# The last group of an MLP pipeline: layer 1 first, three second-layer tiles held back, and a shorter last norm

## The chip, the core and the metric

The kernel runs on one core of a Trainium2 chip. Its time is the time on the device in microseconds (us), a median of several runs. One further execution is recorded by the hardware profiler; the profile and the trace below are of that execution. Engines are named as the profile names them: PE is TensorE (PEld its weight loads), DVE is VectorE, ACT is ScalarE, POOL is GpSimd and SP is SyncE, which only issues transfers here.

## The reference, cut to what matters

The input x has 16 x 512 rows of 512 numbers, 8192 rows in all. Each row is normalized in several ways, the results are put side by side, and a two-layer network with a final norm is added back to x:

```python
h = _ln(x, pw_g[pathway_ids], pw_b[pathway_ids])
h = _ln(h, cp_g[compartment_ids], cp_b[compartment_ids])
t = _ln(x, tm_g[time_steps], tm_b[time_steps])
m, n, r = (x + _mlp_ln(state, ...)[:, None, :] for state in (memory, noise, resource))
s = _ln(x, ms_g[scale_type], ms_b[scale_type])
cat = jnp.concatenate([w[0] * h, w[1] * t, w[2] * m, w[3] * n, w[4] * r, w[5] * s], axis=-1)
# _mlp_ln(cat, ...): silu(cat @ int_W1 + b1) @ int_W2 + b2, then _ln with int_g, int_be
return x + _mlp_ln(cat, int_W1, int_b1, int_W2, int_b2, int_g, int_be)
```

All of it is in float32.

## The kernel before, in words

**Tiling.** The 8192 rows are first ordered by their pair of compartment and scale type, and then go through in 16 groups ("windows") of 512 rows. A group has four tiles of 128 rows. The first layer is folded into three products for each tile, all into one PSUM tile: block X (x itself, with the matrix `wx_` for the three broadcast states), block V (the normalized x, with a matrix for the tile's pair, for t and s together) and block H (the twice normalized h, with `wh_`). So a group is 12 first-layer tile products and 4 second-layer ones. Each is four chunks of the 512-long sum, and each chunk is two PE instructions of 128x512.

**What a group needs.** The V matrix of a tile is made in two steps. `s_part` (line 190) writes four scaled chunks on ACT, and `build` (line 196) adds a scaled second matrix to each chunk on DVE. There are two buffers for these matrices, `vs[0]` and `vs[1]`, used in turn, so the third and fourth tile of a group take the buffers of the first and second once PE has read them, chunk by chunk. Each PE product waits for its chunk alone. The H block comes from the "front": `front_a` (normalized x on ACT, line 237; then DVE lines 260 to 265 and a power on POOL, line 269), `front_b1` (line 147 on DVE, line 276 on ACT) and `front_b2` (line 289 and a blockwise transpose, line 156, on DVE). `spread` then has SP issue 16 transfers (line 164) that lay the transposed blocks out as PE needs them. The hidden values go the same way: `hidden` (add on DVE, line 309; silu on ACT, line 312), `turn_z` (transpose on DVE), `spread`.

**The end of a group.** `layer2` (line 324) is the second product. `last_a` adds the bias on DVE (line 327) and sums the squares on ACT (line 332). `last_std` takes the variance on DVE (line 340) and the power -1/2 on POOL (line 345). `last_b` scales by it and by the gain (line 353), then adds the row (line 354), both on DVE. `put_out` is an indirect transfer issued by POOL (line 358); each one waits until the one before it has landed. The mean needs no work here, because the means of the second matrix's rows were taken out beforehand. `shift_x` (line 294, POOL) adds the norm's offset to the stored x. `gather_add` (line 130, POOL) fetches the first layer's row offsets.

**The order.** It is written out by hand; each engine runs its instructions in the order in which the code gives them. `step(s, older, prev, st, nx, nn)` is one of 16 steps of a group: `st` is the group in its first layer, `prev` the one before it, which is in its second layer, `older` the one before that, whose outputs are being stored. Steps 0 to 3 are the four X tiles, steps 4 to 11 alternate a V tile of `st` with a second-layer tile of `prev`, steps 12 to 15 are the H tiles. The norm of `prev` is finished for all four tiles at once (one power of 128x4) while the H tiles run. After group 15, its own second layer stands alone: `end_hidden` (last hidden tile, transposes, 16 transfers), and then four times `layer2`, `last_a`, `last_std`, `last_b`, `put_out` (lines 990 to 999). There are three buffers for x (`xbs`), used by the groups in turn; PSUM has four tiles for the first layer and four for the second.

Of the kernel before, what the change touches and what calls it, by code (L numbers as in the profile page):

```python
# [8 lines left out]
F32 = mybir.dt.float32  # L9
I32 = mybir.dt.int32  # L10
AF = mybir.ActivationFunctionType
ALU = mybir.AluOpType
AX = mybir.AxisListType

P = 128
# [37 lines left out]
def kernel(ctx: ExitStack, tc: tile.TileContext, a: dict, out: bass.AP):  # L53
# [23 lines left out]
    nc = tc.nc  # L77
    B, S, D = a["x"].shape
    NT = B * S
    NJ = S // P  # L80
    NC = D // P
    NW = NT // S
    Q = 4
# [11 lines left out]
    gp = ctx.enter_context(tc.tile_pool(name="gp", bufs=3))  # L95
# [16 lines left out]
    vs = [const.tile([P, NC, D], F32, name=f"vs{k}") for k in range(2)]  # L112
# [3 lines left out]
    yb = const.tile([P, NJ, D], F32, name="yb")  # L116
    rows = const.tile([P, 3, D], F32, name="rows")
# [11 lines left out]
    def gather(dst, table, idx, **kw):  # L129
        nc.gpsimd.indirect_dma_start(dst, None, table, bass.IndirectOffsetOnAxis(ap=idx, axis=0), **kw)  # L130
# [20 lines left out]
    def rot_tile(blk, name):  # L151
        return catp.tile([P, Q, NC, NJ, L], F32, tag=f"rot{blk}", name=name)

    def turn(rot, j, src):

        nc.vector.transpose(rot[:, :, :, j, :].rearrange("p q c t -> p c q t"),  # L156
                            src.rearrange("p (c q t) -> p c q t", c=NC, q=Q))

    def spread_row(st, rot, cat, blk, g):

        if cat not in st:
            st[cat] = catp.tile([P, Q, NC, P], F32, tag=f"cat{blk}", name=f"{cat}{st['w']}")
        for q in range(Q):
            nc.sync.dma_start(st[cat][q * L : (q + 1) * L, g].rearrange("p c t -> p (c t)"),  # L164
                              st[rot][g * L : (g + 1) * L, q].rearrange("p c j t -> p (c j t)"))

    def spread(st, blk):
        for g in range(Q):
            spread_row(st, "r" + blk, "c" + blk, blk, g)
# [12 lines left out]
        gather(cp, cp_rows[:, :], i_cp[:, j, w : w + 1])  # L182
        st["g", j] = pw, cp

    def s_part(st, g):

        w = st["w"]
        st["v", g] = v = vs[(Q * w + g) % 2]
        for c in range(NC):
            nc.scalar.activation(v[:, c], ws[:, c], AF.Identity, scale=scs[:, c, g, w : w + 1])  # L190

    def build(st, g):
        w = st["w"]
        v = st["v", g]
        for c in range(NC):
            nc.vector.scalar_tensor_tensor(v[:, c], wt[:, c], sct[:, c, g, w : w + 1], v[:, c], ALU.mult, ALU.add)  # L196

    def gather_add(st, g):
        w = st["w"]
        st["add", g] = t = gp.tile([P, D], F32, tag="add", name=f"add{w}_{g}", bufs=4)  # L200
        gather(t, rows_2[:, :], i_add[:, g, w : w + 1])
# [39 lines left out]
    def turn_to(st, rot, blk, j, src):  # L241
        if rot not in st:
            st[rot] = rot_tile(blk, f"{rot}{st['w']}")
        turn(st[rot], j, src)
# [10 lines left out]
    def norm_n(st, j):  # L255
        st["xn", j] = norm(st, j, "rs", "nm", "xn")

    def front_1(st, j):
        pw, _ = st["g", j]
        nc.vector.tensor_mul(pw[:, :D], st.pop(("xn", j)), pw[:, :D])  # L260
        nc.vector.tensor_add(pw[:, :D], pw[:, :D], pw[:, D:])
        st["mv", j] = mv = small.tile([P, 1, 2], F32, tag="mvh", name="mvh")
        stats(mv, 0, pw[:, :D], P, "h")
        st["ve", j] = ve = small.tile([P, 1], F32, tag="veh", name="veh")
        nc.vector.tensor_scalar_add(ve, mv[:, :, 1], EPS)  # L265

    def front_pow(st, j):
        st["rs", j] = rs = small.tile([P, 1], F32, tag="rsh", name="rsh")
        nc.gpsimd.tensor_tensor(rs, st.pop(("ve", j)), mhalf[:, :1], ALU.pow)  # L269

    def front_mean(st, j):
        st["nm", j] = neg_mean(st.pop(("mv", j)), st["rs", j], 1, "h")

    def front_norm(st, j):
        pw, _ = st["g", j]
        nc.scalar.activation(pw[:, :D], pw[:, :D], AF.Identity, bias=st.pop(("nm", j)), scale=st.pop(("rs", j)))  # L276

    def front_a(st, j):
        norm_n(st, j)
        front_1(st, j)  # L280
        front_pow(st, j)

    def front_b1(st, j):
        front_mean(st, j)
        front_norm(st, j)

    def front_b2(st, j):
        pw, cp = st.pop(("g", j))
        nc.vector.tensor_mul(pw[:, :D], pw[:, :D], cp)  # L289
        turn_to(st, "rH", "H", j, pw[:, :D])  # L290

    def shift_x(st, j):

        nc.gpsimd.tensor_add(st["xb"][:, j, :], st["xb"][:, j, :], rows[:, 2, :])  # L294


    def psum(k, name):
        return (ps_1, ps_2)[k].tile([P, D], F32, tag=("p1", "p2")[k], name=name)

    def layer1(st, blk, g):  # L300
        if blk == "X":
            st["p1", g] = psum(0 if st["w"] == 0 else 1, f"p1_{st['w']}_{g}")
        m = {"X": wx_, "V": st.get(("v", g)), "H": wh_}[blk]
        for c in range(NC):
            nc.tensor.matmul(st["p1", g], st["c" + blk][:, g, c, :], m[:, c, :],  # L305
                             start=(blk == "X" and c == 0), stop=(blk == "H" and c == NC - 1))

    def hidden_add(st, g):
        nc.vector.tensor_add(st["add", g], st["p1", g], st["add", g])  # L309

    def hidden_silu(st, g):
        nc.scalar.activation(st["add", g], st["add", g], AF.Silu)  # L312

    def hidden(st, g):
        hidden_add(st, g)
        hidden_silu(st, g)

    def turn_z(st, g):
        turn_to(st, "rZ", "Z", g, st["add", g])

    def layer2(st, j):
        st["p2", j] = p2 = psum(0, f"p2_{st['w']}_{j}")
        for c in range(NC):
            nc.tensor.matmul(p2, st["cZ"][:, j, c, :], w2[:, c, :], start=(c == 0), stop=(c == NC - 1))  # L324

    def last_add(st, j):
        nc.vector.tensor_add(yb[:, j, :], st["p2", j], rows[:, 0, :])  # L327

    def last_sum(st, j):
        if "ssy" not in st:  # L330
            st["ssy"] = small.tile([P, NJ], F32, tag="ssy", name="ssy", bufs=2)
        nc.scalar.activation(junk, yb[:, j, :], AF.Square, accum_out=st["ssy"][:, j : j + 1])  # L332

    def last_a(st, j):
        last_add(st, j)
        last_sum(st, j)

    def last_var(st, lo=0, hi=NJ):
        st["vey"] = ve = small.tile([P, NJ], F32, tag="vey", name="vey")[:, lo:hi]
        nc.vector.tensor_scalar(ve, st["ssy"][:, lo:hi], 1.0 / D, EPS, ALU.mult, ALU.add)  # L340

    def last_pow(st, lo=0, hi=NJ):
        if lo == 0:
            st["rsy"] = small.tile([P, NJ], F32, tag="rsy", name="rsy")
        nc.gpsimd.tensor_tensor(st["rsy"][:, lo:hi], st["vey"], mhalf[:, lo:hi], ALU.pow)

    def last_std(st, lo=0, hi=NJ):
        last_var(st, lo, hi)
        last_pow(st, lo, hi)

    def last_b(st, j):
        y = yb[:, j, :]
        nc.vector.scalar_tensor_tensor(y, y, st["rsy"][:, j : j + 1], rows[:, 1, :], ALU.mult, ALU.mult)  # L353
        nc.vector.tensor_add(y, y, st["xb"][:, j, :])

    def put_out(st, j):
        w = st["w"]
        nc.gpsimd.indirect_dma_start(out_rows, bass.IndirectOffsetOnAxis(ap=tok[:, j, w : w + 1], axis=0),  # L358
                                     yb[:, j, :], None)
# [51 lines left out]
    at = 0  # L411
# [197 lines left out]
    sts = [{"w": w, "xb": xbs[(w + 2) % 3], "tok": (tok, w)} for w in range(NW)] + 2 * [None]  # L609
# [37 lines left out]
    _, bcol = row_col(bpos, NG, "b")  # L647
# [207 lines left out]
    def home(w, blk):  # L855
# [8 lines left out]
    }  # L864
    for_tile = {
        "gx": lambda st, j: gather_x(st, (j,)), "gh": gather_h, "xs": x_sums, "sp": s_part, "bd": build, "nv": norm_v, "tx": turn_x, "xn": norm_n,
        "f1": front_1, "fp": front_pow, "fm": front_mean, "fn": front_norm, "f2": front_b2, "ga": gather_add,
        "ha": hidden_add, "hs": hidden_silu, "tz": turn_z, "l2": layer2, "la": last_add, "lq": last_sum,
        "lb": last_b, "po": put_out, "sh": shift_x,
    }  # L870
# [22 lines left out]
    def end_hidden(st, older):  # L893

        last_b(older, 3)
        hidden(st, 3)
        turn_z(st, 2)
        turn_z(st, 3)
        spread(st, "Z")
# [83 lines left out]
        if s in (5, 6, 7, 8):  # L983
            shift_x(st, s - 5)

    for w in range(2, NW):
        for s in range(16):
            step(s, *sts[w - 2 : w + 3])

    older, prev = sts[NW - 2 : NW]  # L990
    put_out(older, 2)
    end_hidden(prev, older)
    put_out(older, 3)
    for j in range(NJ):
        layer2(prev, j)
        last_a(prev, j)
        last_std(prev, j, j + 1)
        last_b(prev, j)
        put_out(prev, j)


# [51 lines left out]
```

## Time and profile before

The median is 1050.83 us over 3 runs (1048.07 to 1051.16).

| profiled execution of the kernel before | us |
|---|---|
| its own device time | 1051.53 |
| span from its first to its last instruction | 1049.4 |
| PE busy | 998.2 |
| DVE busy | 873.8 |
| ACT busy | 572.8 |
| POOL busy | 568.5 |

The page of a profile gives the busy time of each engine, the span in 40 slices, the groups of instructions with the mean duration of one, and the idle time before them with the instruction that ended it ("<-DMA cZ<-rZ": a transfer from rZ to cZ ended it). Further views of the trace list instructions in order of time ("start, duration, engine, line, operation, output<-input, count [idle before <-releaser]"; "SPq" is a transfer that SP issues), or tell for chosen stretches how busy each engine was, and which TensorE clock was granted as a share of full speed.

### The profile page before, as it was taken

What the parts mean: (1) busy time and instruction counts of PE and PEld (TensorE: products, weight loads), DVE (VectorE), ACT (ScalarE), POOL (GpSimd) and SP (SyncE); (2) the same over time, 40 slices, a digit from 0 to 9 for tenths busy, and PEclk for the clock granted to TensorE, in tenths of its full rate; (3) what the DMA queues carried; (4) which work ended last, traced back from release to release, by engine and by line L of the source; (5) the groups of instructions that cost most, each with busy time, mean ns of one, the idle gap of its engine ahead of it and who ended that gap; (6) DMA issues with size and microseconds to landing.
All of it is one profiled execution on the core that took longest, in us unless ns stands there. A gap on an engine that the chain in (4) does not pass through costs nothing.

```text
span 1049.4 us, 11007 instructions
## 1 busy us (share of the span) xinstructions
PE 998.2 (95%) x2523; PEld 452.1 (43%) x2523; DVE 873.8 (83%) x1574; ACT 572.8 (55%) x1153; POOL 568.5 (54%) x570
## 2 busy tenths in 40 slices
PE   6989699899999999999999999999999999999976
PEld 5634244343344444444444444444444444444432
DVE  8878789888889898888888888888888888898643
ACT  3689774473746474637464646555464737463311
POOL 4764651645656564737464646465655556563412
PEclk9979899899999999999999999999999999999998
DMA  9685887666767585857676666767666767675412
GB/s 282 205 261 161 230 246 223 164 182 184 199 184 211 165 224 153 234 154 221 173 208 173 196 180 202 191 184 191 196 186 195 194 195 196 185 209 145 131 53 67
DMA packets 95655, 197.66 MB, mean 188 GB/s; under 512 B 26290, under 2 KB 26290, under 8 KB 95592
## 3 DMA queue, kind: packets, MB, share of 16 engines
q0 software_dynamic: 32096, 108.55, 35.8%
q1 hardware_dynamic: 62230, 87.44, 29.9%
q10 hardware_dynamic: 1266, 0.99, 0.3%
q8 instruction: 21, 0.34, 0.1%
q14 instruction: 42, 0.34, 0.1%
HBM read 104.14 MB, written 21.44 MB: 120 GB/s over the span
## 4 chain that ended last, share of the span: by engine, by line
PE 78%; DVE 8%; DMA 4%; ACT 4%; issue 3%; SPq 1%; POOL 1%; POOLq 0%; DVEq 0%; ACTq 0%
PE p L305 55%; PE p L324 17%; PE pe L811 3%; PE pn L574 2%; SPq L164 1%; DVE vs L196 1%; ACT vs L190 1%; DMA add<-rows,i_add 1%; DMA xbs<-in_mem_W 1%; PE ph L549 1%; DVE yb L353 1%; ACT pw L276 1%; DMA out<-yb,tok 1%; POOL xbs L130 1%; DVE pw L289 1%
## 5 line engine op out<-in xcount | busy, mean ns | idle before, releaser
L305 PE MATMUL p<-vs,cV 128*128 128x512 f32 x512 | 233.1, 599 | 5.8 <-DVE vs L196 5.8
L324 PE MATMUL p<-w,cZ 128*128 128x512 f32 x512 | 231.5, 597 | 7.1 <-DMA cZ<-rZ 7.1
L305 PE MATMUL p<-wx__82,cX 128*128 128x512 f32 x512 | 227.2, 602 | 2.0 <-DVE add L309 2.0
L305 PE MATMUL p<-wh__83,cH 128*128 128x512 f32 x512 | 222.8, 592 | 0.0
L196 DVE SCALAR_TENSOR_TENSOR vs<-wt,sct,vs 128x512 f32<-128x512 f32 x256 | 209.3, 876 | 0.0
L190 ACT ACTIVATE vs<-ws,scs 128x512 f32<-128x512 f32 x256 | 163.4, 707 | 2.7 <-PE pe L811 2.1
L269 POOL TENSOR_TENSOR rsh<-veh,mhalf 128x1 f32<-128x1 f32 x64 | 45.9, 718 | 203.2 <-DVE veh L265 195.3
L305 PEld LDWEIGHTS p<-vs,cV 128*128 128x128 f32 x512 | 97.7, 192 | 131.9 <-issue 96.8
L324 PEld LDWEIGHTS p<-w,cZ 128*128 128x128 f32 x512 | 98.0, 192 | 131.2 <-issue 130.5
L305 PEld LDWEIGHTS p<-wx__82,cX 128*128 128x128 f32 x512 | 98.7, 193 | 126.7 <-issue 119.5
L305 PEld LDWEIGHTS p<-wh__83,cH 128*128 128x128 f32 x512 | 97.3, 190 | 122.5 <-issue 122.0
L276 ACT ACTIVATE pw<-pw,nmh,rsh 128x512 f32<-128x512 f32 x64 | 51.8, 810 | 130.5 <-DVE nmh L147 130.5
L312 ACT ACTIVATE add<-add 128x512 f32<-128x512 f32 x64 | 40.3, 630 | 145.9 <-DVE add L309 145.9
L358 POOL DMA_INDIRECT out<-yb,tok x64 | 67.8, 1059 | 65.5 <-DVE yb L353 24.3
L332 ACT ACTIVATE junk<-yb 128x512 f32<-128x512 f32 x64 | 40.1, 627 | 98.0 <-DVE yb L327 98.0
L130 POOL DMA_INDIRECT add<-rows,i_add x64 | 75.9, 1186 | 24.2 <-issue 9.2
L260 DVE TENSOR_TENSOR pw<-xn,pw 128x512 f32<-128x512 f32 x64 | 44.0, 688 | 48.5 <-ACT xn L237 48.5
L294 POOL TENSOR_TENSOR xbs<-xbs,rows 128x512 f32<-128x512 f32 x64 | 81.4, 1274 | 0.9
L130 POOL DMA_INDIRECT cp<-cp_rows,i_cp x64 | 67.9, 1061 | 19.5 <-issue 19.2
L130 POOL DMA_INDIRECT xbs<-in_x,tok x64 | 64.9, 1015 | 24.2 <-issue 18.0
L130 POOL DMA_INDIRECT pw<-in_pw,i_pw x64 | 63.9, 999 | 22.4 <-issue 12.7
L237 ACT ACTIVATE xm<-xbs,mnm,mrs 128x512 f32<-128x512 f32 x64 | 48.7, 804 | 40.5 <-DVE rV L156 40.5
(228 smaller groups left out, 1220.5 us busy)
## 6 DMA issues: line engine op xcount, KB each, us to landing
cX<-rX SPq DMA_DIRECT2D x256, 64.0 KB
cV<-rV SPq DMA_DIRECT2D x256, 64.0 KB
cH<-rH SPq DMA_DIRECT2D x256, 64.0 KB
cZ<-rZ SPq DMA_DIRECT2D x256, 64.0 KB
cVe<-rVe SPq DMA_DIRECT2D x64, 64.0 KB
rows<-adde SPq DMA_DIRECT2D x14, 256.0 KB
w1x<-in_int_W SPq DMA_DIRECT2D x2, 1024.0 KB
ws<-in_int_W SPq DMA_DIRECT2D x1, 1024.0 KB
```

The lines of the kernel that those rows point to most:

```text
L130: nc.gpsimd.indirect_dma_start(dst, None, table, bass.IndirectOffsetOnAxis(ap=idx, axis=0), **kw)
L190: nc.scalar.activation(v[:, c], ws[:, c], AF.Identity, scale=scs[:, c, g, w : w + 1])
L196: nc.vector.scalar_tensor_tensor(v[:, c], wt[:, c], sct[:, c, g, w : w + 1], v[:, c], ALU.mult, ALU.add)
L237: nc.scalar.activation(t, st["xb"][:, j, :], AF.Identity, bias=st[nm][:, j : j + 1], scale=st[rs][:, j : j + 1])
L260: nc.vector.tensor_mul(pw[:, :D], st.pop(("xn", j)), pw[:, :D])
L269: nc.gpsimd.tensor_tensor(rs, st.pop(("ve", j)), mhalf[:, :1], ALU.pow)
L276: nc.scalar.activation(pw[:, :D], pw[:, :D], AF.Identity, bias=st.pop(("nm", j)), scale=st.pop(("rs", j)))
L294: nc.gpsimd.tensor_add(st["xb"][:, j, :], st["xb"][:, j, :], rows[:, 2, :])
L305: nc.tensor.matmul(st["p1", g], st["c" + blk][:, g, c, :], m[:, c, :], start=(blk == "X" and c == 0), stop=(blk == "H" and c == NC - 1))
L312: nc.scalar.activation(st["add", g], st["add", g], AF.Silu)
L324: nc.tensor.matmul(p2, st["cZ"][:, j, c, :], w2[:, c, :], start=(c == 0), stop=(c == NC - 1))
L358: nc.gpsimd.indirect_dma_start(out_rows, bass.IndirectOffsetOnAxis(ap=tok[:, j, w : w + 1], axis=0), yb[:, j, :], None)
```

## The change

The steps of the last group (`st` = group 15) are written out in a function of their own, `last_window`. The loop over `step` ends one group earlier.

- The order of PE's tiles in the last group was X X X X, V P V P V P V P, H H H H, then Z Z Z Z (P is a second-layer tile of group 14, Z one of group 15). It becomes X X X X, V V V V, P, H H H H, P P P, Z Z Z Z.
- The V matrix of the third tile is written into the x buffer of group 13, which is no longer needed. That of the fourth goes into the first tile's buffer. On DVE, the builds of the third and fourth matrix follow the front of tile 3 directly; the first of them is issued after the SP transfers for H.
- The last two stores of group 13 stay in steps 1 and 2, but are issued at the head of the step, ahead of the power on POOL instead of behind it. The gathers of the row offsets come in steps 3 to 6 instead of 3, 4, 7, 8, and the four `shift_x` in steps 4 to 7 instead of 5 to 8.
- The transposed hidden values of group 15 use the buffers of block V, since those of block Z still hold group 14's.
- The norm of both last groups is finished tile by tile, by `finish`. A multiplication by the gain (line 994) is placed behind the bias add; a single instruction (line 996) then scales by the power and adds the row. The two instructions of `last_b` depended on the power both.

```diff
-    def s_part(st, g):
+    def s_part(st, g, at=None):
-        st["v", g] = v = vs[(Q * w + g) % 2]
+        st["v", g] = v = vs[(Q * w + g) % 2] if at is None else at
...
-    def turn_z(st, g):
-        turn_to(st, "rZ", "Z", g, st["add", g])
+    def turn_z(st, g, blk="Z"):
+        turn_to(st, "rZ", blk, g, st["add", g])
...
-    for w in range(2, NW):
+    def last_window(older, prev, st):
+
+        def finish(done, j):
+
+            y = yb[:, j, :]
+            layer2(done, j)
+            last_a(done, j)
+            yg = gp.tile([P, D], F32, tag="cp", name=f"yg{done['w']}_{j}")
+            nc.vector.tensor_mul(yg, y, rows[:, 1, :])
+            last_std(done, j, j + 1)
+            nc.vector.scalar_tensor_tensor(y, yg, done["rsy"][:, j : j + 1], done["xb"][:, j, :], ALU.mult, ALU.add)
+            put_out(done, j)
+
+        for s in range(13):
+            if s == 8:
+                finish(prev, 0)
+            if s < 12:
+                layer1(st, "XVH"[s // 4], s % 4)
+            if s == 0:
+                end_hidden(prev, older)
+            elif s == 1:
+                put_out(older, 2)
+                front_a(st, 2)
+                s_part(st, 2, older["xb"])
+            elif s == 2:
+                put_out(older, 3)
+                front_b1(st, 2)
+                front_a(st, 3)
+                front_b2(st, 2)
+            elif s == 3:
+                front_b1(st, 3)
+                build(st, 1)
+                front_b2(st, 3)
+                spread(st, "H")
+                build(st, 2)
+            elif s == 5:
+                s_part(st, 3, vs[Q * st["w"] % 2])
+            elif s == 6:
+                build(st, 3)
+            elif s >= 9:
+                hidden(st, s - 9)
+                if s >= 10:
+                    turn_z(st, s - 10, "V")
+            if 3 <= s < 7:
+                gather_add(st, s - 3)
+            if 4 <= s < 8:
+                shift_x(st, s - 4)
+        turn_z(st, 3, "V")
+        for g in range(Q):
+            spread_row(st, "rZ", "cZ", "V", g)
+        for j in range(1, NJ):
+            finish(prev, j)
+        for j in range(NJ):
+            finish(st, j)
+
+    for w in range(2, NW - 1):
         for s in range(16):
             step(s, *sts[w - 2 : w + 3])
-
-    older, prev = sts[NW - 2 : NW]
-    put_out(older, 2)
-    end_hidden(prev, older)
-    put_out(older, 3)
-    for j in range(NJ):
-        layer2(prev, j)
-        last_a(prev, j)
-        last_std(prev, j, j + 1)
-        last_b(prev, j)
-        put_out(prev, j)
+    last_window(*sts[NW - 3 : NW])
```

## The prediction

> **What bounds the kernel now.** I read the page first, then the last 90 us in order of time, engine by engine.
>
> ```profile
> span 1049.4 us, 11007 instructions
> PE 998.2 (95%) x2523; PEld 452.1 (43%) x2523; DVE 873.8 (83%) x1574; ACT 572.8 (55%) x1153; POOL 568.5 (54%) x570
> PEclk9979899899999999999999999999999999999998
> ...
> L324 PE MATMUL p<-w,cZ 128*128 128x512 f32 x512 | 231.5, 597 | 7.1 <-DMA cZ<-rZ 7.1
> ```
>
> PE is busy 95% of the span. Its second-layer line has one idle time, 7.1 us, ended by the transfer of the transposed hidden values. PE and two stretches of the span in order of time show where:
>
> ```profile
> 1002.27 13.90 PE L305 MATMUL p<-wh__83,cH 128*128 128x512 f32 x32
> 1023.29 7.04 PE L324 MATMUL p<-w,cZ 128*128 128x512 f32 x11 [7.12 <-DMA cZ<-rZ]
> ...
> 1016.00:1020.70 4.70, 0.17 (x1) 0.00 (x0) 2.72 (x5) 0.63 (x1) 1.28 (x2) 1.00 0.21 72
> 1020.70:1027.50 6.80, 4.21 (x5) 1.85 (x6) 0.00 (x0) 0.00 (x0) 0.00 (x0) 0.50 0.55 144
> ```
>
> The last H tile ends near 1016.0; the last four second-layer tiles can't start before 1023.29, and the granted clock (the number behind ACT's and POOL's columns) is 0.50 until 1027.5. Those four tiles are then paced by the norm. DVE and POOL on the last of them:
>
> ```profile
> 1040.39 0.68 DVE L327 TENSOR_TENSOR yb<-p,rows 128x512 f32<-128x512 f32 x1
> 1041.92 0.15 DVE L340 TENSOR_SCALAR vey<-ssy 128x1 f32<-128x1 f32 x1 [0.85 <-ACT junk L332]
> 1042.76 0.75 DVE L353 SCALAR_TENSOR_TENSOR yb<-yb,rsy,rows 128x512 f32<-128x512 f32 x1 [0.69 <-POOL rsy L345]
> 1043.54 0.69 DVE L354 TENSOR_TENSOR yb<-yb,xbs 128x512 f32<-128x512 f32 x1
> ...
> 1044.52 1.01 POOL L358 DMA_INDIRECT out<-yb,tok  x1 [1.80 <-DVE yb L354]
> ```
>
> The four bias adds start at 1029.09, 1032.86, 1036.62 and 1040.39: 3.77 us a tile, where PE needs 3.43 (32 instructions in 13.74). From the last add to the end of the span are 9.03 us.
>
> **The order at the end.** PE's last group starts at 961.07 and ran without a gap up to 1016.0: 16 tiles of 3.434. In the new order 13 tiles stand ahead of the end of H (961.07 + 44.64 = 1005.71), three of the neighbour group follow (1016.01), then the four own ones (1029.75). From the end of H to the first own tile took 1023.29 - 1016.01 = 7.28, with DVE at first busy with the old norm. Three tiles cover 10.30, so 3.0 stay spare, the wait and the half clock are both gone, and the last bias add starts 0.20 behind PE (as at 1002.47, behind the tile ended at 1002.27): 1029.95.
>
> **The norm.** From the bias add to line 353 are 2.37 us (1040.39 to 1042.76), set by squares, variance and power. The new multiplication, 0.69 by line 354's row, fits into DVE's 0.85 wait for the squares. Then one instruction of 0.75 instead of 0.75 and 0.69. A tile takes 3.12 on DVE, less than PE's 3.43, so PE sets the pace. Behind the last add: 3.12, then 0.29 to POOL (1044.23 to 1044.52) and 4.88 to the end, 8.3 in all against 9.03. Each store waits for the one before to land; issue to landing is 3.1 in the median, and the new stores are 3.43 apart, so this holds narrowly and costs some tenths if not. The eight powers, four more than before, stay in POOL's idle time. End: 1029.95 + 8.3 = 1038.25. Saved so far: 1049.4 - 1038.25 = **11.15 us**.
>
> **What is brought forward.** Three moves look free. The third tile's four scaled chunks go to ACT at 967.25, where it idles 3.53 before line 276; four of them took 2.55, so 0.9 is spare, and beyond that the H front would be late by the excess. The two stores of group 13 go ahead of a power on POOL: the first can't be issued before the one at 964.51 has landed (about 967.6) and takes 1.0, the power is due at 969.99; without that gap the front waits for it. The H transfers need some 4.4 us for the first rows (for the hidden values SP's first is at 1018.90, PE starts at 1023.29) and are now due at PE's tenth tile instead of its thirteenth, about 995 against an issue near 982. SP has nothing else.
>
> The builds are not free. DVE and POOL in order of time, and the durations of lines 196 and 294:
>
> ```profile
> 976.22 2.73 DVE L196 SCALAR_TENSOR_TENSOR vs<-wt,sct,vs 128x512 f32<-128x512 f32 x4
> 978.86 0.68 DVE L289 TENSOR_TENSOR pw<-pw,cp 128x512 f32<-128x512 f32 x1
> 979.58 0.71 DVE L156 STREAM_TRANSPOSE rH<-pw 128x512 f32<-128x512 f32 x1
> 981.87 0.69 DVE L327 TENSOR_TENSOR yb<-p,rows 128x512 f32<-128x512 f32 x1 [1.58 <-PE p L324]
> 982.48 4.33 DVE L196 SCALAR_TENSOR_TENSOR vs<-wt,sct,vs 128x512 f32<-128x512 f32 x4
> ...
> 978.80 1.59 POOL L130 DMA_INDIRECT add<-rows,i_add  x1 [0.30 <-issue]
> 980.40 2.50 POOL L294 TENSOR_TENSOR xbs<-xbs,rows 128x512 f32<-128x512 f32 x2
> 983.06 1.23 POOL L130 DMA_INDIRECT add<-rows,i_add  x1 [0.16 <-issue]
> 984.32 1.27 POOL L294 TENSOR_TENSOR xbs<-xbs,rows 128x512 f32<-128x512 f32 x1
> ...
> L196 DVE SCALAR_TENSOR_TENSOR vs<-wt,sct,vs x12: 737/744/2101, 976.2 to 991.3; 128x512 f32<-128x512 f32 x12
> ...
> L294 POOL TENSOR_TENSOR xbs<-xbs,rows x64: 1250/1274/1298, 191.5 to 987.0; 128x512 f32<-128x512 f32 x64
> ```
>
> A build of four takes 2.73 alone, and 4.33 when shifts of x run beside it: the one chunk over which a whole shift lay took 2.10 instead of 0.74, 1.36 more. The shift never shows it (1.25 to 1.30 over all 64). In the old order the first two shifts fell where DVE waited for PE (979.6 to 981.87), and the second-layer tile between two V tiles gave a late build 3.43 us. Both covers go: V tiles now follow each other, and POOL, rid of the store at 976.10, is 1.3 us earlier.
>
> New order on POOL: gathers near 976.1 and 977.5; shift 978.65 to 979.95; gather; shift 981.35 to 982.6; gather; two shifts 984.05 to 986.55. On DVE: the first build's last chunk and line 289 are pushed to about 981.1, the transpose (not held: it shows 0.71 throughout) to 981.75. Then chunk by chunk of the third matrix: 983.2, 983.85, and behind the two shifts 987.1, 987.8; of the fourth: 988.45, 989.1, 989.75, 990.4. PE wants the third tile's chunks at 981.67 and each 0.86: it waits **1.5** for the first and **2.2** for the third; the fourth tile then finds its chunks 0.3 early. Sum 3.7. If the second gather takes the 1.59 of the row above, all of it comes 0.5 later and the same steps give 2.0 + 2.2 = 4.2.
>
> By the Trainium skill ("SBUF — State Buffer", "SBUF: two separate sides") the port shared by GpSimd and a VectorE instruction with two SBUF inputs goes to whichever starts first, for its whole length. The trace differs: the run of four ends at 986.81, its last chunk takes 0.74 and overlaps by 0.08, so the chunk of 2.10 started near 984.05, 0.27 ahead of the shift at 984.32, and was still the one held. By the rule, a running chunk would finish and the shift wait; redoing the steps I get 0.6 + 1.0 + 1.9 = 3.5. Either way about the same. Bounds: 0, if the shifts fall on transposes and bias adds (PSUM input, 0.69 beside shifts too); 4.9, if every shift costs 1.36 and the gathers are slow. I take **3.8**, from the row.
>
> The other rule speaks against the change: "TensorE: Matmul & The Clock Gate" ("What's actually happening") has the clock halved after one idle window of about 3.4 us. In this trace the 7.28 us gap brought 6.8 us of half clock, and near 247 a wait booked as 2.02 us (3.0 between the starts of two weight loads) brought 3.4 us of 0.51; a 1.13 us one at 271 none. By the rule, waits of 1.5 and 2.2 with 1.7 of work between cost nothing more; by the second row they may cost one half-clock window, 1.7 us. I take nothing, and keep 1.7 to 3.4 for the range.
>
> **Sum.** 11.15 - 3.8 = 7.35 saved. The profiled execution would go from 1051.53 to 1044.2, the median, 0.70 below it, from 1050.83 to **1043.5**.
>
> **The rivals.**
> - *The collision costs little* (0 to 1.5): 1039.7 to 1041.2. For it: the phase of the shifts is mine, not measured. Against: all four shifts lie within the 10 us in which DVE has 6.8 us of two-input work due.
> - *The waits also halve the clock* once or twice: 1045.2 to 1046.9.
> - *Slower*: the clock stays at half through the H tiles and the tail. Each 3.43 us tile at half clock costs 3.43 more, so the saving of 7.35 is used up after 14.7 us of half clock; with all 13 tiles behind the V block it would be 1050.83 - 7.35 + 44.6 = 1088. Against: behind the preparation, the longest such stretch here is 6.8 us.
> - *It doesn't close the gap*: the own hidden values arrive after the three held-back tiles. It needs the 7.28 us chain to be over 10.3; within 0.3% of no change only if it is over 14.5. DVE and SP are idle there.
>
> **How the numbers follow.** 0.60 for the forecast (1042 to 1045.5), 0.17 for little collision, 0.15 for the halved clock, 0.05 for slower, 0.03 for the gap that stays. A difference under about 0.3% (3.15 us) can't be told from none here. Faster: 0.60 + 0.17 + 0.15 = 0.92; same 0.03; slower 0.05. The range runs from the lower end of little collision to the upper end of the halved clock, 1039.5 to 1047; what it leaves out are the last two cases and the runs' own spread.
>
> **What would show it.** Right: no PE idle before line 324; clock 1.0 to the end of PE; two PE waits on line 196 of 1 to 2.5 us after the second V tile; chunks of 2.1 us or longer; line 327 about 3.4 apart at the end; 8.3 us behind the last one. Wrong: V tiles without waits, more than 5 us of them, or an idle time before the own second-layer tiles.

## The result, and the profile after

The changed kernel takes 1045.81 us in the median of 22 runs (1042.35 to 1049.85), the kernel before 1049.28 over the 22 runs beside them (1043.98 to 1054.92). The ratio is 0.9965, with a 95% interval from 0.9951 to 0.998: 3.7 us faster, between 2.1 and 5.1. The forecast was a median of 1043.5, 7.35 us faster.

The page of the changed kernel:

```profile
span 1043.4 us, 11015 instructions
PEclk9979999899999999999999999999999999999998
...
L324 PE MATMUL p<-w,cZ 128*128 128x512 f32 x512 | 228.9, 592 | 0.0
```

The second layer has no idle time any more (7.1 us before), and its instructions take 592 ns in the mean instead of 597. PE's last group, in order of time:

```profile
960.05 13.90 PE L305 MATMUL p<-wx__82,cX 128*128 128x512 f32 x32
973.78 7.17 PE L305 MATMUL p<-vs,cV 128*128 128x512 f32 x16
982.52 1.98 PE L305 MATMUL p<-xbs,cV 128*128 128x512 f32 x4 [1.57 <-DVE xbs L196]
986.43 1.98 PE L305 MATMUL p<-xbs,cV 128*128 128x512 f32 x4 [1.93 <-DVE xbs L196]
988.25 3.60 PE L305 MATMUL p<-vs,cV 128*128 128x512 f32 x8
991.69 3.60 PE L324 MATMUL p<-w,cZ 128*128 128x512 f32 x8
995.12 13.90 PE L305 MATMUL p<-wh__83,cH 128*128 128x512 f32 x32
1008.85 24.20 PE L324 MATMUL p<-w,cZ 128*128 128x512 f32 x56
```

The last seven tiles run as one piece, so the gap is closed. Two waits have appeared in the third V tile. Eight unbroken tiles would have brought PE to 960.05 + 27.47 = 987.52; it got there at 991.69, so the V tiles cost **4.17 us**.

The span shrank by 6.0 us, but 1.0 of that is not the change's: this group starts at 960.05 here and at 961.07 in the profile before, after the same instructions. Over all the profiles below its start lies between 954.72 and 961.57. So I compare **the stretch** from the start of the last group's X tiles to the end of the span: 1049.4 - 961.07 = 88.3 us before, 1043.4 - 960.05 = 83.4 after. That is 5.0 us shorter, inside the interval of the timed runs.

DVE and POOL beside the V tiles:

```profile
975.67 4.10 DVE L196 SCALAR_TENSOR_TENSOR vs<-wt,sct,vs 128x512 f32<-128x512 f32 x4
979.70 0.68 DVE L289 TENSOR_TENSOR pw<-pw,cp 128x512 f32<-128x512 f32 x1
980.41 0.71 DVE L156 STREAM_TRANSPOSE rH<-pw 128x512 f32<-128x512 f32 x1
981.04 5.99 DVE L196 SCALAR_TENSOR_TENSOR xbs<-wt,sct,xbs 128x512 f32<-128x512 f32 x4
986.96 2.73 DVE L196 SCALAR_TENSOR_TENSOR vs<-wt,sct,vs 128x512 f32<-128x512 f32 x4
...
977.92 1.29 POOL L294 TENSOR_TENSOR xbs<-xbs,rows 128x512 f32<-128x512 f32 x1
980.64 1.27 POOL L294 TENSOR_TENSOR xbs<-xbs,rows 128x512 f32<-128x512 f32 x1
983.33 2.49 POOL L294 TENSOR_TENSOR xbs<-xbs,rows 128x512 f32<-128x512 f32 x2
```

The first build has one shift over it (4.10), the second three (5.99), the third none (2.73). Whatever DVE's line 196 loses stands beside a shift. The tail, the last tile on DVE and the last three stores on POOL, with the time from a store's issue to its landing over the last seven:

```profile
1033.63 0.68 DVE L327 TENSOR_TENSOR yb<-p,rows 128x512 f32<-128x512 f32 x1
1034.35 0.69 DVE L994 TENSOR_TENSOR yg<-yb,rows 128x512 f32<-128x512 f32 x1
1035.17 0.15 DVE L340 TENSOR_SCALAR vey<-ssy 128x1 f32<-128x1 f32 x1
1036.56 0.75 DVE L996 SCALAR_TENSOR_TENSOR yb<-yg,rsy,xbs 128x512 f32<-128x512 f32 x1 [1.24 <-POOL rsy L345]
...
1031.23 1.10 POOL L358 DMA_INDIRECT out<-yb,tok  x1 [1.92 <-DVE yb L327]
1034.85 1.09 POOL L358 DMA_INDIRECT out<-yb,tok  x1 [1.92 <-DVE yb L327]
1035.96 0.57 POOL L345 TENSOR_TENSOR rsy<-vey,mhalf 128x1 f32<-128x1 f32 x1
1038.45 1.03 POOL L358 DMA_INDIRECT out<-yb,tok  x1 [1.93 <-issue]
...
DMA to landing us min/median/max: 2.8/2.8/2.9
```

The variance is ready at 1035.32, but its power starts at 1035.96, since POOL's queue holds the store of the tile before it, which itself waited. The wait for the power is 1.24 instead of 0.69, the stores are 3.6 apart, and from the last bias add to the end of the span are 9.77 us, where the sum had 8.3.

### The profile page after: what moved, and what is told of

It is laid out like the page before. It is cut to its first block, busy times and chain, and to the rows that moved or that the text cites. A ratio compares the mean times of both kernels' runs of the same rounds, so it can differ in the third digit from the quotient of the medians.

```text
span 1043.4 us, 11015 instructions
## 1 busy us (share of the span) xinstructions
PE 994.1 (95%) x2523; PEld 450.3 (43%) x2523; DVE 877.9 (84%) x1577; ACT 572.7 (55%) x1153; POOL 572.2 (55%) x573
## 4 chain that ended last, share of the span: by engine, by line
PE 70%; DVE 11%; DMA 4%; ACT 4%; issue 4%; SPq 3%; POOL 2%; POOLq 0%; DVEq 0%; ACTq 0%
PE p L305 48%; PE p L324 16%; SPq L164 3%; PE pe L811 3%; DVE vs L196 3%; PE pn L574 2%; DVE pw L289 1%; DMA xbs<-in_mem_W 1%; ACT vs L190 1%; ACT pw L276 1%; DVE add L309 1%; DVE yb L353 1%; DMA add<-rows,i_add 1%; POOL xbs L130 1%; DVE pw L260 1%
## 5 line engine op out<-in xcount | busy, mean ns | idle before, releaser
L305 PE MATMUL p<-vs,cV 128*128 128x512 f32 x504 | 229.6, 600 | 5.6 <-DVE vs L196 5.6
L324 PE MATMUL p<-w,cZ 128*128 128x512 f32 x512 | 228.9, 592 | 0.0
L196 DVE SCALAR_TENSOR_TENSOR vs<-wt,sct,vs 128x512 f32<-128x512 f32 x252 | 206.3, 877 | 0.0
L190 ACT ACTIVATE vs<-ws,scs 128x512 f32<-128x512 f32 x252 | 160.7, 707 | 2.6 <-PE pe L811 2.1
```

## The experiments

My theory after this comparison has two parts: POOL's shifts hold the builds (4.2 us), and the chain of stores, each waiting for the landing of the one before, holds the tail (2.0 us). Rivals: the builds are late for another reason; DVE's added multiplication or the order on POOL slows the tail.

**Shifts moved behind the builds** (`e1_shift_late`).

```diff
-            if 4 <= s < 8:
-                shift_x(st, s - 4)
+            if s >= 9:
+                shift_x(st, s - 9)
```

> The changed kernel with one edit: the four shifts of x on POOL move from the V tiles to the H tiles, behind the first held store. From the start of the last group's X tiles to the end of the span the kernel before has 88.35 us and the changed one 83.37. Theory (the shifts hold the builds on DVE): PE's two waits in the V tiles, 4.17 us against an unbroken run, go to under 0.3; the builds take 2.73 us each; the stretch becomes about 79.2, and the kernel is some 9 us faster than the one before instead of 4 to 5. Rival (DVE has too much to do there, or the third matrix in a borrowed buffer is late for a reason of its own): the waits stay at 3 us or more and the stretch at 83.

Measured: ratio 0.9897 (0.9862 to 0.9931), 10.8 us faster than the kernel before (9.5 between the medians). Its PE, DVE and POOL:

```profile
957.69 13.90 PE L305 MATMUL p<-wx__82,cX 128*128 128x512 f32 x32
971.42 7.03 PE L305 MATMUL p<-vs,cV 128*128 128x512 f32 x16
978.29 3.60 PE L305 MATMUL p<-xbs,cV 128*128 128x512 f32 x8
981.72 3.60 PE L305 MATMUL p<-vs,cV 128*128 128x512 f32 x8
...
977.33 2.70 DVE L196 SCALAR_TENSOR_TENSOR xbs<-wt,sct,xbs 128x512 f32<-128x512 f32 x4
979.94 2.73 DVE L196 SCALAR_TENSOR_TENSOR vs<-wt,sct,vs 128x512 f32<-128x512 f32 x4
...
993.27 4.94 POOL L294 TENSOR_TENSOR xbs<-xbs,rows 128x512 f32<-128x512 f32 x4
```

No wait is left in the V tiles, the builds take 2.7 each, the shifts run where DVE has bias adds from PSUM and transposes. The stretch is 1036.8 - 957.69 = 79.1, as the theory had it. The borrowed buffer has no part in the delay. By its ratio this is the fastest version here that computes everything.

**Every second store to another tensor** (`e2_two_targets`).

```diff
+    other = dram.tile([NT, D], F32, name="other")
-    def put_out(st, j):
+    def put_out(st, j, to=None):
-        nc.gpsimd.indirect_dma_start(out_rows, bass.IndirectOffsetOnAxis(ap=tok[:, j, w : w + 1], axis=0),
+        nc.gpsimd.indirect_dma_start(out_rows if to is None else to, bass.IndirectOffsetOnAxis(ap=tok[:, j, w : w + 1], axis=0),
...
-            put_out(done, j)
+            put_out(done, j, other[:, :] if j % 2 else None)
```

> The changed kernel with the second and fourth tile of the last two groups stored to a scratch tensor in DRAM instead of the output (those four tiles' output is left out), so that a store no longer waits for the landing of the one issued just before it. Number, size and place of the stores are the same. Theory (the chain of stores paces the tail): bias adds 3.43 us apart to the end, 8.3 us behind the last one instead of 9.8, the last add 0.2 us behind PE instead of 0.7; the stretch from 83.37 to about 81.4. Rival (the added multiplication or the powers pace it): adds stay 3.6 apart and the stretch within 0.5 of 83.4.

Measured: ratio 0.9921 (0.989 to 0.9951). The last two bias adds and the last store:

```profile
1026.45 0.69 DVE L328 TENSOR_TENSOR yb<-p,rows 128x512 f32<-128x512 f32 x1 [0.29 <-PE p L325]
1029.88 0.69 DVE L328 TENSOR_TENSOR yb<-p,rows 128x512 f32<-128x512 f32 x1 [0.30 <-PE p L325]
...
1033.31 1.03 POOL L359 DMA_INDIRECT other<-yb,tok  x1 [1.08 <-DVE yb L997]
```

The adds are 3.43 apart and wait for PE alone; from the last to the end of the span (1038.2) are 8.3. The stretch is 1038.2 - 956.92 = 81.3, 2.0 shorter with the same work in the same places. The store chain is the loss in the tail, and the multiplication costs nothing.

**Both at once** (`e3_late_two_targets`): the two edits above together.

> Both edits: shifts of x beside the H tiles, and every second store of the last two groups to a scratch tensor (their output is left out). This is the forecast's sum without its loss: 88.35 - 11.15 = 77.2 us for the stretch, if collision and store chain are all that the sum lacked. If one of them only hides the other, the two gains (about 4.2 and 2.0) don't add, and the stretch stays above 78.

Measured: ratio 0.9878 (0.9845 to 0.9911); the stretch is 1031.9 - 954.72 = 77.2. The two losses add up, and together they are all that the sum of 11.15 lacked.

**The old end of the norm in the new order** (`e4_old_norm`).

```diff
-            yg = gp.tile([P, D], F32, tag="cp", name=f"yg{done['w']}_{j}")
-            nc.vector.tensor_mul(yg, y, rows[:, 1, :])
             last_std(done, j, j + 1)
-            nc.vector.scalar_tensor_tensor(y, yg, done["rsy"][:, j : j + 1], done["xb"][:, j, :], ALU.mult, ALU.add)
+            last_b(done, j)
```

> The changed kernel with the old end of the norm: power, then scaling by power and gain, then the row's addition (two instructions behind the power on DVE). My sum gave the new end 0.3 us a tile and 0.7 at the end, some 2.5 us in all. If the store chain sets 3.6 us a tile anyway, the old end's 3.77 costs little: the stretch goes from 83.37 to 84 to 84.5. If DVE's part was worth what the sum said, it goes to about 86.

Measured: ratio 0.9961 (0.9936 to 0.9986); the stretch is 1041.2 - 957.18 = 84.0. So the new end of the norm is worth 0.6 us in this kernel, not 2.5: a tile on DVE takes 3.77 without it (bias adds at 1024.57, 1028.34 and 1032.11), a store 3.6 with it.

**The new end of the norm in the old order** (`e5_norm_alone`).

```diff
+        yg = gp.tile([P, D], F32, tag="cp", name=f"yg{prev['w']}_{j}")
+        nc.vector.tensor_mul(yg, yb[:, j, :], rows[:, 1, :])
         last_std(prev, j, j + 1)
-        last_b(prev, j)
+        nc.vector.scalar_tensor_tensor(yb[:, j, :], yg, prev["rsy"][:, j : j + 1], prev["xb"][:, j, :], ALU.mult, ALU.add)
```

> The kernel before, with nothing changed but the end of the norm in the four tiles behind the loop: gain beside the squares, then one instruction for power and row. From the start of the last group's X tiles to the end of the span the kernel before has 88.35 us. If the chain of stores sets the pace (3.6 us a store where DVE's old end needed 3.77), the stretch becomes about 87.1. By my sum's step (PE paces, 3.43 a tile, 8.3 behind the last add) it becomes about 86. Rival (the added multiplication is in the way): no change or longer.

Measured: ratio 0.9993 (0.9976 to 1.001), which doesn't tell it from no change. The profile does: the stretch is 1047.7 - 960.66 = 87.0, 1.3 shorter. Here the bias adds are 3.43 apart (1032.16, 1035.59, 1039.02), the stores 3.54 (1035.69, 1039.22, 1042.77). With only four stores the delay grows to 0.3 and doesn't reach DVE.

**No tile held back** (`e6_none_held`).

```diff
             if s == 8:
-                finish(prev, 0)
+                for j in range(NJ):
+                    finish(prev, j)
...
-        for j in range(1, NJ):
-            finish(prev, j)
```

> The changed kernel with all four second-layer tiles of the neighbour group ahead of the H tiles, none held back. Theory (the three held tiles are what covers the hidden values' way back): PE idles 6.7 to 6.9 us before the own second-layer tiles, the clock is halved for some 7 us as before, and the stretch goes from 83.35 to 90 to 91, longer than the 88.35 of the kernel before, since the waits in the V tiles stay and are no longer paid for. Rival (DVE, freed of the old norm, gets the hidden values back much sooner): an idle time of 4 us or less and a stretch of 85 to 86.

Measured: ratio 1.0025 (1.001 to 1.0041), slower than the kernel before. PE in order of time, and two stretches with the granted clock (behind ACT's and POOL's columns):

```profile
983.75 1.98 PE L305 MATMUL p<-xbs,cV 128*128 128x512 f32 x4 [1.57 <-DVE xbs L196]
987.67 3.68 PE L305 MATMUL p<-xbs,cV 128*128 128x512 f32 x4 [1.93 <-DVE xbs L196]
...
1028.42 15.82 PE L324 MATMUL p<-w,cZ 128*128 128x512 f32 x32 [6.18 <-DMA cZ<-rZ]
...
984.20:987.60 3.40, 1.54 (x4) 0.38 (x2) 3.40 (x3) 0.00 (x0) 2.83 (x3) 1.00 0.73 181
987.60:991.10 3.50, 3.43 (x4) 1.43 (x5) 3.33 (x6) 0.00 (x0) 0.00 (x0) 0.53 0.38 90
```

The stretch is 1052.9 - 961.26 = 91.6 (expected 90 to 91), and the gap is back with 6.18 us (expected 6.7 to 6.9): the held tiles are the cover, and DVE's freedom takes less than 1 us off the gap. Something else shows here. The V tiles wait 1.57 and 1.93, as in the changed kernel, but this time the clock is halved for one window. The second half of the third V tile takes 3.68 instead of 1.98, and that is 1.7 of the 91.6.

**POOL's additions doubled** (`e7_adds_doubled`).

```diff
                 shift_x(st, s - 4)
+                nc.gpsimd.tensor_add(junk, rows[:, 0, :], rows[:, 2, :])
```

> The changed kernel with one more POOL addition of the same size behind each of the four shifts (of two constant rows, into a buffer that nothing reads). If a POOL addition simply holds every two-input DVE instruction for its length, the builds end about 4.9 us later, PE's loss in the V tiles goes from 4.17 to 9.0 us in three waits (about 1.2, 3.1 and 4.7), and the stretch from 83.35 to 88.2; the longest wait may also halve the clock, which would add 1.7 to 3.4. Rival (the builds are late for a reason of their own): under 1 us more.

Measured: ratio 1.0015 (1.0 to 1.003); the stretch is 1051.3 - 961.57 = 89.7. PE in order of time, and three stretches:

```profile
982.43 1.13 PE L305 MATMUL p<-vs,cV 128*128 128x512 f32 x2 [0.95 <-DVE vs L196]
986.34 3.68 PE L305 MATMUL p<-xbs,cV 128*128 128x512 f32 x4 [2.78 <-DVE xbs L196]
992.67 3.27 PE L305 MATMUL p<-xbs,cV 128*128 128x512 f32 x4 [2.66 <-DVE xbs L196]
...
999.63 3.60 PE L324 MATMUL p<-w,cZ 128*128 128x512 f32 x8
...
986.00:989.50 3.50, 3.16 (x4) 1.14 (x4) 3.50 (x3) 0.00 (x0) 3.48 (x3) 0.56 0.64 165
989.50:993.00 3.50, 0.84 (x2) 0.30 (x2) 3.50 (x2) 0.00 (x0) 2.56 (x3) 0.95 0.47 116
993.00:996.40 3.40, 3.40 (x5) 1.30 (x4) 2.93 (x5) 0.00 (x0) 0.00 (x0) 0.53 0.24 58
```

The ratio hardly tells it from the kernel before, but well from the changed kernel (0.9965, at most 0.998). The V tiles now lose 999.63 - 961.57 - 27.47 = 10.6 us. Of the two half-clock windows, the first is hidden in the next wait. Beside the second, the last 12 instructions take 6.96 us (992.67 to 999.63) where 12 of 0.43 would take 5.15, so some 1.8 are the clock's and 8.8 the holds' (expected 9.0). Four more additions of 1.27 cost PE 4.6 us without the clock. So the hold lasts as long as POOL adds, whatever the operands. A gather on POOL did not hold: in the changed kernel a chunk of line 196 lay wholly beside the gather at 982.07 and took its usual 0.74.

**Powers ahead of the stores** (`e8_power_first`, on top of `e1_shift_late`). Each store is kept back until the next tile's power has been issued.

```diff
+        held = []
+
+        def store_held():
+            while held:
+                put_out(*held.pop())
...
             last_std(done, j, j + 1)
+            store_held()
...
-            put_out(done, j)
+            held.append((done, j))
```

> The kernel with the shifts beside the H tiles (stretch 79.1), and on POOL each tile's power ahead of the store of the tile before it, so that no power stands behind a waiting store. If the landing of one store is what the next one waits for, the bias adds go back to 3.43 apart and 0.2 behind PE, but the stores stay 3.5 to 3.7 apart or more and the stretch is 79.1 to 79.8, no shorter, since each store is also issued later. If the power queued behind a store is what paces the tail, the stretch falls to about 78.

Measured: ratio 0.9924 (0.99 to 0.9949); the stretch is 1039.4 - 959.18 = 80.2, 1.1 longer than in `e1_shift_late`. The bias adds are 3.43 apart and wait for PE, so DVE is free of the chain. The stores are 3.98, 3.04, 3.44, 3.39, 3.44 and 3.91 apart, so the expected 3.5 or more came only at both ends. The last two, and DVE beside the first of them:

```profile
1030.42 0.75 DVE L1003 SCALAR_TENSOR_TENSOR yb<-yg,rsy,xbs 128x512 f32<-128x512 f32 x1 [0.69 <-POOL rsy L345]
...
1030.67 1.40 POOL L358 DMA_INDIRECT out<-yb,tok  x1 [0.28 <-DMA out<-yb,tok]
1034.58 0.97 POOL L358 DMA_INDIRECT out<-yb,tok  x1 [2.51 <-issue]
```

The end was expected at 79.1 to 79.8, so it is a little worse than expected. Each store is now issued a tile later: the last one's data are ready at 1031.17, but the store before it started only at 1030.67, and the last has to wait until 1034.58. So this order on POOL frees DVE and pays for it with a later last store. It doesn't show that the step from store to store has a fixed length; that the chain is the loss in the tail rests on `e2_two_targets` and `e3_late_two_targets`. Five of the seven issues take 1.36 to 1.52 instead of about 1.0. These five start 0.14 to 0.28 us after line 1003 on DVE (line 996 of the changed kernel), the other two later; no run moves that instruction, so the cause is argued, not shown.

## Why the prediction was right and where it missed

- **The gap and its cover: right.** No idle time before line 324, clock 1.0 to the end of PE. Without held tiles the gap is back.
- **The collision: right, 0.4 too small.** The forecast named two waits in the third V tile, 1.5 and 2.2 us (or 2.0 and 2.2), and took 3.8; PE lost 4.17. Every part of it is there: the first build's last chunk held, the third matrix late in its first and third chunk, the fourth in time. Moving the shifts takes it away, doubling the additions takes it to 8.8 and the clock.
- **The shared port.** The forecast preferred the row (a running chunk is held by a later shift) to the rule of the Trainium skill ("SBUF — State Buffer", "SBUF: two separate sides"), under which the first to start keeps the port. The changed kernel repeats the row: a chunk that began 0.27 ahead of a shift took 2.12, and the shift kept its 1.29. But I read too much into the row: it doesn't contradict the rule. In the profiles before and after, all 59 chunks of line 196 with a shift over them end 0.56 us after the last such shift ends, whether their record starts up to 0.34 ahead of a shift or up to 0.85 behind it. So a chunk recorded ahead of a shift had no more of its work done than one recorded behind it, and the recorded start doesn't tell who had the port first. The time can't decide either, since the rule, as I applied it, gave 3.5.
- **The step that failed is "The norm".** I wrote that each store waits for the landing of the one before, that 3.1 against 3.43 "holds narrowly and costs some tenths if not". It cost 2.0 us: 0.5 because the last bias add stood 0.74 behind PE instead of 0.20, and 1.5 behind it (9.77 instead of 8.3). What the term left out is the time from a landing to the next issue. The last stores land 2.8 to 2.9 us after their issue, and follow each other 3.6 apart, so some 0.7 lie between; beside the 16 transfers of the hidden values the first two steps were even 4.05 (1015.92, 1019.97, 1024.02). I compared the landing with the tile and not the whole step. And I gave the power POOL's "idle time", though it is queued behind the waiting store; from there the delay reached DVE.
- **The sum closes.** 88.3 - 7.35 would have been 81.0. Add 0.4 for the collision and 2.0 for the stores: 83.4, as measured. With both taken away the stretch is 77.2 = 88.35 - 11.15.
- **The clock: left at nothing, rightly for the profiled execution.** I kept 1.7 for one half-clock window in the range, from the row near 247. The profile without held tiles has exactly that, behind the same two waits. The rule of the Trainium skill ("TensorE: Matmul & The Clock Gate", "What's actually happening") asks for an idle window of about 3.4 us; PE had 1.5 us of work in the 3.4 us before the clock fell. Three profiles with these waits (the changed kernel, `e2_two_targets`, `e4_old_norm`) show no drop, one does.
- **What decides the drop.** In all ten profiles the changes of the clock lie whole multiples of 3.41 us apart, so each trace can be divided into lengths of 3.41 us by them. From 100 us on, the clock was halved after all 45 full-clock lengths with less than 1.40 us of PE work in them, after none of the 2645 with more than 1.49, and after two of the five between. The leanest length beside the waits, in the changed kernel, in `e2_two_targets` and in `e6_none_held` (PE's busy time is the first number behind the comma):

```profile
982.28:985.70 3.42, 1.98 (x4) 0.67 (x4) 3.42 (x3) 0.00 (x0) 3.40 (x3) 1.00 0.66 182
...
981.57:984.98 3.41, 1.75 (x4) 0.86 (x5) 3.41 (x4) 0.00 (x0) 1.05 (x1) 1.00 0.59 157
...
984.37:987.78 3.41, 1.48 (x5) 0.49 (x4) 3.41 (x2) 0.00 (x0) 2.66 (x3) 1.00 0.72 180
```

The same two waits leave 1.98, 1.75 or 1.48 in a length, as the division falls, and 1.48 is on the border. At 44% of the places where the division could fall, the changed kernel's trace has a length with 1.49. So at most some four in ten timed runs may pay the 1.7, about 0.7 us in the mean; this is an estimate from that trace. How often the changed kernel pays it in its timed runs was not measured. It may be part of why they gained 3.7 and the stretch 5.0, and so may the spread of the runs; that stays open.

The time was inside the range and the sign right; the gain was half of what I forecast. That the time was inside is in part luck: the range was reckoned from 1050.83, and the kernel before ran in 1049.28 beside the changed one. The measured ratio on 1050.83 gives 1047.2, just above the range's end of 1047.

## What to carry to other kernels

When work is moved forward on one engine, list what the neighbour that shares its SBUF port does in those microseconds: here four GpSimd additions of 1.27 us took 4.2 of 11 us, and the 4.2 came back whole when the additions were moved to a stretch in which VectorE reads PSUM or transposes. For a chain of transfers that wait for each other, count a step as issue, landing and restart together (3.5 to 3.6 us at the end of the kernel here, not 2.9) before you compare it with the tile; a faster engine in front of it gains only what lies above that step. And ask which other instruction stands behind the waiting one in its queue.

## What I had not expected of the hardware

- A store that had to wait for a landing was issued some 0.7 us after it; one that had only its data to wait for, 0.3 us after them (1033.02 to 1033.31 with two targets). In `e8_power_first` five stores were issued 0.3 us after the landing too, each just behind a power on POOL; what the 0.7 consists of stays open.
- Two PE waits of 1.57 and 1.93 us with 1.7 us of work between can halve the clock for 3.4 us in one profile and not in three others: what counts is how much PE work falls into a 3.41 us length, and that shifts from one execution to the next.
- The same instructions bring the last group to its start anywhere between 954.72 and 961.57 us. Differences of a few us in a tail are read from the tail's own stretch, not from the span.
